# Fetched rows completed straight from the matmul accumulator, a deeper ring of gather buffers and a new order at the start of a two-layer graph attention kernel

## The chip, the cores and the metric

The kernel runs on one core of one Trainium2 chip. A core has a matrix engine (TensorE, in the rows PE for its matmuls and PEld for its weight loads), a vector engine (VectorE, DVE), a scalar engine (ScalarE, ACT), a general engine that also issues the indirect transfers (GpSimd, POOL), an engine that issues most other transfers (SyncE, SP) and 16 DMA engines. Each engine works through its own list of instructions in order, and they wait for each other by semaphores. Matmuls write to PSUM, an accumulator memory; everything else on the chip lies in SBUF. The metric is the device time of one execution in microseconds (us).

## The reference

N = 6250 nodes of 768 numbers, E = 100000 directed edges sorted by their destination, plus one self-loop per node. Cut to what matters:

```python
def gat_conv(x, src, dst, W, a_src, a_dst, bias, heads):
    h = (x @ W).reshape(n, heads, -1)
    alpha_s = (h * a_src[None]).sum(-1)
    alpha_d = (h * a_dst[None]).sum(-1)
    e = leaky_relu(alpha_s[src] + alpha_d[dst], 0.2)
    e = exp(e - segment_max(e, dst)[dst])
    alpha = e / (segment_sum(e, dst)[dst] + 1e-16)
    return segment_sum(h[src] * alpha[:, :, None], dst).reshape(n, -1) + bias

h = relu(layernorm(x))
h = relu(gat_conv(h, src, dst, W1, a_src1, a_dst1, b1, 4))   # 768 -> 256, 4 heads
h = relu(gat_conv(h, src, dst, W2, a_src2, a_dst2, b2, 1))   # 256 -> 256, 1 head
return x + relu(h @ Wm1 + bm1) @ Wm2 + bm2                   # 256 -> 768
```

All of it is float32.

## The kernel before

**Phase 1 (nodes).** The nodes lie in 49 tiles of 128. For each tile the kernel loads x (and for most tiles x transposed; the tiles in TURNED are transposed on the chip instead), takes means and variances (`moments`), spreads the means by a small matmul (`spread_means`), subtracts them (`centre`) and multiplies by W1 with 12 matmuls (L516). The row of a node (256 features and some factors, 268 numbers) stays in SBUF in `kept[tile]` for the whole layer and is also stored to a table in DRAM (L543).

**Layers (edges).** The edges stand in pairs of 2 x 128, two pairs to a group g, 196 groups to a layer. For every 128 edges GpSimd issues one indirect DMA that fetches their source rows from the table into one half of a buffer `G` (L718). The buffers form a ring, 20 deep. VectorE makes a one-hot matrix per group (`hot`, L746), the edge factors, and the product of rows and factors (`hw`: L796, L806, L808 in layer 1; L796, L799, L803 in layer 2). TensorE sums the edges of a destination with matmuls `o_ps` (L820). In layer 1 VectorE also makes the masks (L735) that layer 2 reads back. Layer 2 has the same form and ends with the two dense layers (y, L1190). When the sums of a node tile are complete, its row for layer 2 replaces the old one in `kept` and goes to the second table (L1074).

**Early rows.** While phase 1 still computes tiles, GpSimd already fetches rows for 30 pairs of layer 1 (SOON: pair i is fetched when the first SOON[i] tiles are in the table; `soon_rows`, L314, 60 indirect DMAs). Sources whose tile is not there yet get a row that is multiplied by zero later (`soon_ok`, from `soon_places`, L305 and L306, two small VectorE instructions per pair). The newest 16 of these buffers (SOON_HELD) stay in the ring; when one more is fetched, the oldest goes to DRAM (`soon_away`, L321). Before layer 1 all the rest follow, and `soon_back` reads each back when its turn comes. The rows that were not there are added in layer 1 from `kept`: VectorE compares the sources with node numbers (`soon_hits`, L338, up to 8 tiles in one instruction, called a part here), TensorE multiplies these matrices by the tiles of `kept` into one PSUM tile called `missing` (`soon_missing`, L351, two matmuls per tile; there is one such PSUM tile), ScalarE copies the sum to SBUF (`soon_out`, L356, into `soon_m`, three of them), and VectorE computes row * soon_ok + soon_m in place (`soon_whole`, L361). Between the layers the same is done for 10 pairs of layer 2 with names that begin with `next` (L381, L414, L420, L425).

**What sets the order.** The order on each engine is that of the code. In layer 1 each iteration g does, for VectorE, the `hot` of the group, at times a mask or a `mine`, then the steps that the table SOON_DOES holds for g, in the order of SOON_ORDER, then the edges of the pairs. SOON_DOES is made from SOON_GROUP: the group `at` in which a pair is used, and before it one part per group. For each of the two halves k of the pair, part j has its `hits` in group g-1 and its `missing` in group g; after the last part, `out` stands in group g+1 and both `whole` stand in group `at`. Towards the end of a layer the ring is made to skip buffers and GpSimd may be only two groups ahead (L941).

Of the kernel before, what the change touches and what calls it, by code (L numbers as in the profile page):

```python
# [17 lines left out]
P = 128  # L18
# [32 lines left out]
SOON_FROM, SOON_HELD = min(SOON), 16  # L51
# [3 lines left out]
TURNED = frozenset({0, 1, 31, 32, 34, 35, 37, 38, 40, 41, 43, 44, 46, 47})  # L55
# [15 lines left out]
for i, at in enumerate(SOON_GROUP):  # L71
    todo = [(2 * i + t, k) for t in range(2) for k in range(len(portions(SOON[i])))]
    for j, (k, part) in enumerate(todo):
        g = at - 1 - len(todo) + j
        SOON_DOES.setdefault(g - 1, []).append(("hits", k, part))
        SOON_DOES.setdefault(g, []).append(("missing", k, part))
        if part == len(portions(SOON[i])) - 1:
            SOON_DOES.setdefault(g + 1, []).append(("out", k, part))
            SOON_DOES.setdefault(at, []).append(("whole", k, part))
    SOON_DOES.setdefault(max(at - 5 - len(todo), 0), []).append(("sources", i, 0))  # L80
SOON_ORDER = ("whole", "out", "missing", "hits", "sources")
# [12 lines left out]
def kernel(  # L94
# [56 lines left out]
    nc.vector.tensor_copy(iota_ps, iota)  # L151
    nc.vector.tensor_copy(nid_ps, nid)
# [84 lines left out]
    def edge_places(ones):  # L237
# [3 lines left out]
        nc.sync.dma_start(src_i, src_cols)  # L241
        yield
        yield
        soonest = sorted(range(len(SOON)), key=SOON.__getitem__)
        for i in range(0, len(SOON), 2):
            for k in soonest[i:i + 2]:
                soon_places(k)
            yield
        for to, of in ((dst_i, dst_cols), (dri, dst_rows)):
            nc.sync.dma_start(to, of)  # L250
            yield
            yield
# [28 lines left out]
    gp = edges_stack.enter_context(tc.tile_pool(name="gathered", bufs=2 * (AHEAD + 2)))  # L281
# [16 lines left out]
    soon_G, soon_of, soon_p, soon_hit, soon_m = {}, {}, {}, {}, {}  # L298
# [55 lines left out]
    def soon_out(pool, k):  # L354
        soon_m[k] = pool.tile([P, TW[1]], F32, name="soon_m", bufs=3)
        nc.scalar.activation(soon_m[k], soon_p.pop(k), AF.Copy)  # L356

    def soon_whole(G, k):
        i, t = divmod(k, 2)
        row = G[soon_pair[i]][:, t]  # L360
        nc.vector.scalar_tensor_tensor(row, row, soon_ok[:, i, t:t + 1], soon_m.pop(k),  # L361
                                       ALU.mult, ALU.add)
# [4 lines left out]
    next_G, next_of, next_p, next_hit, next_m = {}, {}, {}, {}, {}  # L367
# [49 lines left out]
    def next_out(pool, i, t):  # L417

        next_m[i, t] = pool.tile([P, TW[2]], F32, name="next_m", bufs=2)
        nc.scalar.activation(next_m[i, t], next_p.pop((i, t)), AF.Copy)  # L420

    def next_whole(G, i, t):

        row = G[next_pair[i]][:, t]
        nc.vector.scalar_tensor_tensor(row, row, next_ok[:, i, t:t + 1], next_m.pop((i, t)),  # L425
                                       ALU.mult, ALU.add)

    def next_steps(g, pool, sm, G):

        for i, at in enumerate(NEXT_GROUP):  # L430
            if g == at - 10:
                next_sources(pool, i)
            for t in range(2):
# [5 lines left out]
                if g == first + 1:  # L439
                    next_out(sm, i, t)  # L440
                if g == at:
# [4 lines left out]
    with tc.tile_pool(name="w1p", bufs=1) as wp, tc.tile_pool(name="x1", bufs=6) as xp, \  # L446
# [62 lines left out]
        def features1(i):  # L509
# [3 lines left out]
            for k in range(KI):  # L513
                if (i, k) == (1, 2):
                    spread_means(2)
# [41 lines left out]
        nc.sync.dma_start(w1[:, :, :HID], W1.rearrange("(k p) f -> p k f", p=P))  # L557
        for i in range(1, 5):
# [13 lines left out]
        for i in range(NT):  # L572
# [5 lines left out]
            elif i == 1:  # L578
                centre(2)
                moments(3)  # L580
                spread_means(3)
                moments(4)
            else:
                if i + 3 < NT:
                    moments(i + 3)
                if i + 2 < NT:
                    spread_means(i + 2)
                if i + 1 < NT:
                    centre(i + 1)
# [22 lines left out]
            if i >= 10:  # L612
# [922 lines left out]
```

## Time and profile before

| | |
|---|---|
| median of 3 runs | 2086.26 us (2085.61 to 2087.27) |
| profiled execution, its own time | 2083.7 us |
| its span in the profile | 2081.8 us |
| TensorE busy (matmul) | 1767.1 us, 85% |
| VectorE busy | 1496.6 us, 72% |
| GpSimd busy | 1531.1 us, 74% |
| ScalarE busy | 453.6 us, 22% |
| phase 1 | 0 to about 171 us |
| layer 1 (first and last L718 there) | 170.93 to 1081.54 us |
| layer 2 (first L718) | from 1107.75 us |

How to read it: the shares are averages over stages that have different limits. GpSimd is the only engine whose list is full of one kind of instruction (L718), and these stand in a fixed order, so its position at a few places (first gather of phase 1, of layer 1, of layer 2) tells how far the whole program has come. Which engine waits for which in between is read from the waits, and how far one engine runs ahead of another from the time line.

### The profile page before, as it was taken

The numbers are of one execution on the slowest core, as the hardware profiler recorded it, in microseconds if no ns is written. First come the engines' busy times: TensorE is split into PE (matmuls) and PEld (weight loads), VectorE is DVE, ScalarE is ACT, GpSimd is POOL, SyncE is SP. The second block draws the span as 40 slices with busy tenths as digits, with TensorE's granted clock in tenths as the row PEclk, the third lists the DMA queues.
The fourth block names the chain that finished last, engine by engine and source line by source line (L and its number), as shares of the span: only waits on it lengthen the run. The fifth ranks groups of instructions, "written<-read, shape, count | busy, mean of one in ns | idle before, by whom it ended". The sixth has DMA issues, their size and how long they took to land.

```text
span 2081.8 us, 28821 instructions
## 1 busy us (share of the span) xinstructions
PE 1767.1 (85%) x8572; PEld 1335.8 (64%) x8574; DVE 1496.6 (72%) x4344; ACT 453.6 (22%) x1415; POOL 1531.1 (74%) x1669
## 2 busy tenths in 40 slices
PE   8985799999999999988874788887787787787777
PEld 7874687878888888766553555555555555554544
DVE  7845898989889999999973665665665565565554
ACT  5762111111111111222220111111111111111111
POOL 7267777777777777777777777777777777777774
PEclk9997999999999999998986898999999988898989
DMA  9999666666666666666659466556566556556553
GB/s 342 320 324 341 185 169 194 187 180 179 191 174 194 184 182 186 193 194 186 194 123 271 129 180 189 169 178 190 167 180 190 170 178 190 172 175 182 170 180 112
DMA packets 174908, 405.46 MB, mean 195 GB/s; under 512 B 37192, under 2 KB 61983, under 8 KB 174743
## 3 DMA queue, kind: packets, MB, share of 16 engines
q0 software_dynamic: 75040, 210.90, 38.6%
q1 hardware_dynamic: 98332, 191.14, 26.3%
q10 hardware_dynamic: 1370, 1.48, 0.3%
q8 instruction: 72, 1.18, 0.2%
q14 instruction: 94, 0.76, 0.1%
HBM read 334.24 MB, written 69.14 MB: 194 GB/s over the span
## 4 chain that ended last, share of the span: by engine, by line
PE 38%; DMA 20%; DVE 19%; issue 13%; POOL 9%; ACT 0%; DVEq 0%; SPq 0%; POOLq 0%; ACTq 0%
DMA G<-table,src_i 16%; PE o_ps L820 14%; PE missing L351 11%; POOL G L718 8%; PE h_ps L516 4%; PE y_ps L1190 4%; DVE hw L808 4%; DVE hot L746 3%; DVE soon_hit L338 2%; DVE iota_ps L796 2%; DVE hw L803 2%; DVE iota_ps L806 2%; DMA xTt<-in_xT 1%; DVE acc L831 1%; PE h_ps L1067 1%
## 5 line engine op out<-in xcount | busy, mean ns | idle before, releaser
L718 POOL DMA_INDIRECT G<-table,src_i x1484 | 1414.6, 953 | 452.1 <-issue 318.4
L820 PE MATMUL o_ps<-G,hw 128*128 128x258 f32 x1564 | 457.4, 425 | 208.6 <-DVE hw L803 206.0
L820 PEld LDWEIGHTS o_ps<-G,hw 128*128 128x128 f32 x1564 | 302.3, 207 | 338.2 <-DVE hw L803 280.8
L820 PE MATMUL o_ps<-hw,hot 128*128 128x260 f32 x1564 | 415.6, 407 | 65.5 <-DVE hw L808 62.8
L796 DVE TENSOR_TENSOR iota_ps<-G,iota_ps 128x8 f32<-128x8 f32 (+1 forms) x782 | 130.0, 166 | 398.4 <-DMA G<-table,src_i 387.6
L351 PE MATMUL missing<-kept,soon_hit 128*128 128x268 f32 x1648 | 398.4, 393 | 0.0
L820 PEld LDWEIGHTS o_ps<-hw,hot 128*128 128x128 f32 x1564 | 301.5, 199 | 145.4 <-DVE hw L808 91.4
L840 ACT ACTIVATE sum<-acc 32x260 f32<-32x260 f32 (+1 forms) x384 | 160.0, 417 | 1034.7 <-DVE acc L831 969.7
L351 PEld LDWEIGHTS missing<-kept,soon_hit 128*128 128x128 f32 x1648 | 310.7, 191 | 55.2
L803 DVE TENSOR_SCALAR hw<-iota_ps,dcol,w 128x128 f32<-128x128 f32 x782 | 284.9, 406 | 14.4
L808 DVE TENSOR_TENSOR hw<-G,iota_ps 128x520 f32<-128x520 f32 x391 | 272.0, 696 | 27.1
L1190 PE MATMUL y_ps<-wm,mT 128*128 128x384 f32 x392 | 183.2, 598 | 0.0
L516 PE MATMUL h_ps<-w,r 128*128 128x264 f32 (+1 forms) x588 | 140.0, 391 | 8.4 <-ACT r L506 8.1
L746 DVE TENSOR_TENSOR hot<-iota_ps,dcol 128x512 f32<-128x512 f32 x196 | 133.4, 681 | 0.0
L338 DVE TENSOR_TENSOR soon_hit<-soon_of,iota_ps 128x896 f32<-128x896 int32 (+6 forms) x126 | 128.0, 1016 | 2.4 <-PE missing L351 2.4
L516 PEld LDWEIGHTS h_ps<-w,r 128*128 128x128 f32 x588 | 109.5, 193 | 29.1 <-ACT r L506 9.6
L1190 PEld LDWEIGHTS y_ps<-wm,mT 128*128 128x128 f32 x392 | 78.1, 221 | 54.8 <-issue 29.2
L314 POOL DMA_INDIRECT G<-table,soon_i x60 | 57.9, 965 | 61.9 <-DMA table<-kept 41.3
L831 DVE SCALAR_TENSOR_TENSOR acc<-acc,keep,o_ps 128x260 f32<-128x260 f32 (+1 forms) x192 | 91.3, 476 | 0.9 <-PE o_ps L820 0.9
L356 ACT ACTIVATE soon_m<-missing 128x268 f32<-128x268 f32 x60 | 23.7, 394 | 264.5 <-PE missing L351 264.4
L806 DVE TENSOR_TENSOR iota_ps<-iota_ps,G 128x8 f32<-128x8 f32 x391 | 68.1, 174 | 13.4
L799 DVE TENSOR_TENSOR w<-iota_ps,G 128x2 f32<-128x2 f32 x391 | 62.2, 159 | 13.3
(424 smaller groups left out, 1369.9 us busy)
## 6 DMA issues: line engine op xcount, KB each, us to landing
xt<-in_x SPq DMA_DIRECT2D x96, 384.0 KB
drow<-dmod_d SPq DMA_DIRECT2D x49, 512.0 KB
mask_d<-mask SPq DMA_DIRECT2D x97, 256.0 KB
mask<-mask_d SPq DMA_DIRECT2D x97, 256.0 KB
G<-table,src_i POOLq DMA_INDIRECT x1484
out<-y SPq DMA_DIRECT2D x48, 384.0 KB
xTt<-in_xT SPq DMA_DIRECT2D x35, 384.0 KB
soon_d<-G SPq DMA_DIRECT2D x30, 268.0 KB
```

Source lines behind the costliest of these rows:

```text
L338: nc.vector.tensor_tensor(soon_hit[k, part][:, :b - a], soon_of[i][:, t * P:(t + 1) * P].unsqueeze(1).to_broadcast([P, b - a, P]), nid_ps[ ...
L351: nc.tensor.matmul(soon_p[k], hit[:, T - a], kept[T], start=(T == there), stop=(T == NT - 1))
L516: nc.tensor.matmul(h_ps[:, :n], r[:, k], w1[:, k, :n], start=(k == 0), stop=(k == KI - 1))
L718: nc.gpsimd.indirect_dma_start(out=G[k // 2][:n, k % 2], out_offset=None, in_=table[layer], in_offset=bass.IndirectOffsetOnAxis(ap=src_i[: ...
L746: nc.vector.tensor_tensor(hot[g][:, T[0]:T[0] + n], iota_ps.unsqueeze(1).to_broadcast([P, n, P]), dcol[:, k:k + n].unsqueeze(2).to_broadca ...
L796: nc.vector.tensor_mul(v, e2, v)
L803: nc.vector.tensor_scalar(hw[:, t], iota_ps, dcol[:, k:k + 1], w[:, t], ALU.is_equal, ALU.mult)
L808: nc.vector.tensor_mul(hw, Gp[:, :, :RW[1]].rearrange("p t (h c) -> p t h c", h=H), w.unsqueeze(3).to_broadcast([P, 2, H, C + 1]))
L820: nc.tensor.matmul(o_ps[u], l, r[:, :RW[layer]], start=(g % 2 == 0 and k == 0), stop=(g % 2 == 1 and k == tiles(g)[-1]))
L831: nc.vector.scalar_tensor_tensor(acc, run[0], keep[:, u % 2:u % 2 + 1], o_ps.pop(u), ALU.mult, ALU.add)
L840: nc.scalar.activation(done[t][r], acc[r], AF.Copy)
L1190: nc.tensor.matmul(y_ps, mT[:, j], wm2[:, j, s * half:(s + 1) * half], start=False, stop=(j == KH - 1))
```

## The change

- `soon_out` and `next_out` are removed. `soon_whole` and `next_whole` read the PSUM tile directly, and stand in group g+1 after the last part of their half (where `out` stood), no longer in group `at`.
- The ring of G has 24 buffers where it had 20, and SOON_HELD is 21 where it was 16.
- TURNED gets tiles 26 to 30 and 36 and loses 31, 35 and 37: 17 tiles are turned on the chip where 14 were, so 32 loads of x transposed are left of 35.
- W1 is loaded in two halves with the load of tile 1 between; the first six tiles have a new order of `centre`, `moments` and `spread_means`; two copies into PSUM move from the start to tile 5; the loads of the edge lists and with them `soon_places` start some tiles earlier (from i = 7 where it was 10).

```diff
-SOON_FROM, SOON_HELD = min(SOON), 16
+SOON_FROM, SOON_HELD = min(SOON), 21
-TURNED = frozenset({0, 1, 31, 32, 34, 35, 37, 38, 40, 41, 43, 44, 46, 47})
+TURNED = frozenset({0, 1, *range(26, 31), 32, 34, 36, 38, 40, 41, 43, 44, 46, 47})
...
         if part == len(portions(SOON[i])) - 1:
-            SOON_DOES.setdefault(g + 1, []).append(("out", k, part))
-            SOON_DOES.setdefault(at, []).append(("whole", k, part))
+            SOON_DOES.setdefault(g + 1, []).append(("whole", k, part))
...
-SOON_ORDER = ("whole", "out", "missing", "hits", "sources")
+SOON_ORDER = ("whole", "missing", "hits", "sources")
...
-    gp = edges_stack.enter_context(tc.tile_pool(name="gathered", bufs=2 * (AHEAD + 2)))
+    gp = edges_stack.enter_context(tc.tile_pool(name="gathered", bufs=24))
...
-    def soon_out(pool, k):
-        soon_m[k] = pool.tile([P, TW[1]], F32, name="soon_m", bufs=3)
-        nc.scalar.activation(soon_m[k], soon_p.pop(k), AF.Copy)
...
     def soon_whole(G, k):
         i, t = divmod(k, 2)
         row = G[soon_pair[i]][:, t]
-        nc.vector.scalar_tensor_tensor(row, row, soon_ok[:, i, t:t + 1], soon_m.pop(k),
+        nc.vector.scalar_tensor_tensor(row, row, soon_ok[:, i, t:t + 1], soon_p.pop(k),
                                        ALU.mult, ALU.add)
...
                 if g == first + 1:
-                    next_out(sm, i, t)
-                if g == at:
                     next_whole(G, i, t)
...
-        nc.sync.dma_start(w1[:, :, :HID], W1.rearrange("(k p) f -> p k f", p=P))
-        for i in range(1, 5):
+        for h in range(2):
+            ks = slice(h * (KI // 2), (h + 1) * (KI // 2))
+            nc.sync.dma_start(w1[:, ks, :HID], W1.rearrange("(k p) f -> p k f", p=P)[:, ks])
+            if h == 0:
+                fetch_x(1)
+        for i in range(2, 5):
...
                 spread_means(1)
                 centre(1)
                 moments(2)
-            elif i == 1:
-                centre(2)
-                moments(3)
-                spread_means(3)
-                moments(4)
+                spread_means(2)
+            elif i < 4:
+                centre(i + 1)
+                moments(i + 2)
+                spread_means(i + 2)
+                if i == 3:
+                    moments(6)
             else:
+                if i + 1 < NT:
+                    centre(i + 1)
+                if i + 2 < NT:
+                    spread_means(i + 2)
                 if i + 3 < NT:
                     moments(i + 3)
-                if i + 2 < NT:
-                    spread_means(i + 2)
-                if i + 1 < NT:
-                    centre(i + 1)
...
-            if i >= 10:
+            if i >= 7:
                 next(pieces, None)
```

VectorE of before around group 90 of layer 1, the last group but one before pair 183 (half k = 27 of the early rows) is used; `mine` is a node tile's own rows times their self-loop factors:

```order
L746 TENSOR_TENSOR hot<-iota_ps,dcol 128x512
L1038 TENSOR_TENSOR mine<-kept_137,own 128x260
L796 TENSOR_TENSOR iota_ps<-G,iota_ps 128x8
L806 TENSOR_TENSOR iota_ps<-iota_ps,G 128x8
L808 TENSOR_TENSOR hw<-G,iota_ps 128x520
```

The same engine and place of the changed kernel (its line numbers are about 11 lower):

```order
L735 TENSOR_TENSOR hot<-iota_ps,dcol 128x512
L1027 TENSOR_TENSOR mine<-kept_135,own 128x260
L350 SCALAR_TENSOR_TENSOR G<-G,soon_ok,missing_6005 128x268
L785 TENSOR_TENSOR iota_ps<-G,iota_ps 128x8
L795 TENSOR_TENSOR iota_ps<-iota_ps,G 128x8
L797 TENSOR_TENSOR hw<-G,iota_ps 128x520
```

The completion of k = 27 now stands ahead of the two `hw` of this group, and reads `missing`.

VectorE of before one group later, group 91:

```order
L1044 TENSOR_TENSOR all__6197<-mine,sum 128x260
L1057 RECIPROCAL rden<-all__6197 128x4
L1059 TENSOR_TENSOR o<-all__6197,rden 128x256
L746 TENSOR_TENSOR hot<-iota_ps,dcol 128x512
L735 TENSOR_SCALAR mask<-drow,pidx 128x1024
L361 SCALAR_TENSOR_TENSOR G<-G,soon_ok,soon_m 128x268 x2
L338 TENSOR_TENSOR soon_hit<-soon_of,iota_ps 128x768
```

The same in the changed kernel:

```order
L1033 TENSOR_TENSOR all__6159<-mine,sum 128x260
L1046 RECIPROCAL rden<-all__6159 128x4
L1048 TENSOR_TENSOR o<-all__6159,rden 128x256
L735 TENSOR_TENSOR hot<-iota_ps,dcol 128x512
L724 TENSOR_SCALAR mask<-drow,pidx 128x1024
L331 TENSOR_TENSOR soon_hit<-soon_of,iota_ps 128x768
```

Both completions are gone from group 91. The other half of the pair (k = 26) is completed three groups earlier, in group 87.

SyncE of before at the end of phase 1; `soon_d` is the place in DRAM for the early rows, `mask_d` that for the masks:

```order
L321 DMA soon_d<-G 128x536
L543 DMA table_97<-kept_162 128x268
L543 DMA table_97<-kept_163 128x268
L1026 DMA w_2137<-in_W 128x2x256
L194 DMA w2T<-in_W2T 128x2x256
L675 DMA drow<-dmod_d 128x2048 x3
L321 DMA soon_d<-G 128x536 x16
L675 DMA drow<-dmod_d 128x2048
L737 DMA mask_d<-mask 128x1024 x4
```

The same in the changed kernel:

```order
L314 DMA soon_d<-G 128x536
L523 DMA table_95<-kept_160 128x268
L523 DMA table_95<-kept_161 128x268
L1015 DMA w_2148<-in_W 128x2x256
L191 DMA w2T<-in_W2T 128x2x256
L664 DMA drow<-dmod_d 128x2048 x3
L314 DMA soon_d<-G 128x536 x21
L664 DMA drow<-dmod_d 128x2048
L726 DMA mask_d<-mask 128x1024 x4
```

Of the 30 stores of early rows 9 are left inside phase 1 where 14 were, and 21 stand ahead of the first stores of masks where 16 did. The order on GpSimd is the same in both kernels.

## Rows read from the trace of the kernel before

**Rows 1.** Position of GpSimd: time line (start, duration, [idle before <- ended by]).

```profile
88.54 1.14 POOL L314 DMA_INDIRECT G<-table,soon_i  x1 [37.73 <-DMA table<-kept]
...
111.00 0.94 POOL L314 DMA_INDIRECT G<-table,soon_i  x1 [2.32 <-DMA table<-kept]
...
150.78 0.94 POOL L314 DMA_INDIRECT G<-table,soon_i  x1 [4.49 <-DMA soon_d<-G]
...
170.93 0.95 POOL L718 DMA_INDIRECT G<-table,src_i  x1 [0.30 <-issue]
...
1082.71 0.95 POOL L381 DMA_INDIRECT G<-table,next_i  x1 [0.30 <-issue]
...
1107.75 0.95 POOL L718 DMA_INDIRECT G<-table,src_i  x1 [0.30 <-issue]
```

**Rows 2.** Costliest groups of the page: busy, mean ns | idle before.

```profile
L718 POOL DMA_INDIRECT G<-table,src_i x1484 | 1414.6, 953 | 452.1 <-issue 318.4
L351 PE MATMUL missing<-kept,soon_hit 128*128 128x268 f32 x1648 | 398.4, 393 | 0.0
L831 DVE SCALAR_TENSOR_TENSOR acc<-acc,keep,o_ps 128x260 f32<-128x260 f32 (+1 forms) x192 | 91.3, 476 | 0.9 <-PE o_ps L820 0.9
L356 ACT ACTIVATE soon_m<-missing 128x268 f32<-128x268 f32 x60 | 23.7, 394 | 264.5 <-PE missing L351 264.4
```

**Rows 3.** Busy time by stage (layer 1 from 300 us, layer 2).

```profile
core 0: us, PE busy (x) PEld busy (x) DVE busy (x) ACT busy (x) POOL busy (x), PEclk, DMA share, GB/s
300.00:1085.00 785.00, 739.88 (x3773) 604.89 (x3773) 715.55 (x1810) 152.88 (x538) 595.73 (x622) 0.97 0.65 183
1108.00:2082.00 974.00, 764.61 (x3541) 520.04 (x3542) 556.25 (x1958) 171.40 (x457) 722.51 (x762) 0.90 0.59 175
```

**Rows 4.** What VectorE waited for, 240 to 900 us: total, times, longest.

```profile
DVE G L361 <- ACT soon_m L356: 15.7, 7, 3.8
DVE soon_hit L338 <- PE missing L351: 2.4, 3, 1.0
```

**Rows 5.** Time line of VectorE, groups 90 and 91.

```profile
615.46 0.42 DVE L1038 TENSOR_TENSOR mine<-kept,own 128x260 f32<-128x260 f32 x1
...
620.20 0.49 DVE L361 SCALAR_TENSOR_TENSOR G<-G,soon_ok,soon_m 128x268 f32<-128x268 f32 x1
623.90 0.50 DVE L361 SCALAR_TENSOR_TENSOR G<-G,soon_ok,soon_m 128x268 f32<-128x268 f32 x1 [3.21 <-ACT soon_m L356]
...
625.78 0.70 DVE L808 TENSOR_TENSOR hw<-G,iota_ps 128x520 f32<-128x520 f32 x1
...
627.65 0.69 DVE L808 TENSOR_TENSOR hw<-G,iota_ps 128x520 f32<-128x520 f32 x1
```

**Rows 6.** ScalarE at the end of the matmuls of k = 27.

```profile
623.47 0.39 ACT L356 ACTIVATE soon_m<-missing 128x268 f32<-128x268 f32 x1 [8.65 <-PE missing L351]
```

**Rows 7.** TensorE after them.

```profile
623.27 3.67 PE L820 MATMUL o_ps<-hw,hot 128*128 128x260 f32 x16
```

**Rows 8.** End of layer 1 on VectorE, and the start of layer 2 there.

```profile
1084.72 0.70 DVE L808 TENSOR_TENSOR hw<-G,iota_ps 128x520 f32<-128x520 f32 x1
...
1115.53 0.17 DVE L796 TENSOR_TENSOR iota_ps<-G,iota_ps 128x2 f32<-128x2 f32 x1 [17.35 <-DMA G<-table,src_i]
```

**Rows 9.** What VectorE waited for, 200 to 300 us.

```profile
DVE iota_ps L796 <- DMA G<-table,src_i: 6.1, 6, 3.2
```

**Rows 10.** What VectorE waited for, 170 to 200 us.

```profile
DVE mask L735 <- DMA mask_d<-mask: 5.8, 1, 5.8
```

**Rows 11.** TensorE at tile 3 of phase 1.

```profile
19.72 2.86 PE L516 MATMUL h_ps<-w,r 128*128 128x256 f32 x12 [1.95 <-ACT r L506]
```

**Rows 12.** VectorE and GpSimd in phase 1, 45 to 46 us.

```profile
45.71 0.16 DVE L305 TENSOR_SCALAR soon_ok<-src_i 128x2 f32<-128x2 int32 x1
45.79 1.19 POOL L530 TENSOR_TENSOR ha<-kept,a1b 128x512 f32<-128x512 f32 x1
45.90 1.10 DVE L306 TENSOR_TENSOR soon_i<-src_i,soon_ok 128x2 int32<-128x2 int32 x1
```

More of the change, by code (lines that the diff above doesn't have):

```diff
@@ L150 @@
     iota_ps, nid_ps = both_ps[:, :P], both_ps[:, P:P + NT]
-    nc.vector.tensor_copy(iota_ps, iota)
-    nc.vector.tensor_copy(nid_ps, nid)
     eps_c = const.tile([P, 1], F32, name="eps_c")
@@ L240, in edge_places @@
         dri = ones.tile([NCH, CH], I32, name="dri")
-        nc.sync.dma_start(src_i, src_cols)
-        yield
-        yield
+        for to, of in ((src_i, src_cols), (dst_i, dst_cols), (dri, dst_rows)):
+            nc.sync.dma_start(to, of)
+            yield
         soonest = sorted(range(len(SOON)), key=SOON.__getitem__)
@@ L247, in edge_places @@
                 soon_places(k)
[L248 to L251, printed above, removed]
             yield
@@ L297 @@
     soon_d = dram.tile([len(SOON), P, 2 * TW[1]], F32, name="soon_d")
-    soon_G, soon_of, soon_p, soon_hit, soon_m = {}, {}, {}, {}, {}
+    soon_G, soon_of, soon_p, soon_hit = {}, {}, {}, {}
     soon_pair = {i: pair for pair, i in SOON_AT.items()}
@@ L366 @@
     next_d = dram.tile([len(NEXT), P, 2, TW[2]], F32, name="next_d")
-    next_G, next_of, next_p, next_hit, next_m = {}, {}, {}, {}, {}
+    next_G, next_of, next_p, next_hit = {}, {}, {}, {}
     next_pair = {i: pair for pair, i in NEXT_AT.items()}
@@ L415, in next_missing @@
                              stop=(T == NT - 1))
-    def next_out(pool, i, t):
-        next_m[i, t] = pool.tile([P, TW[2]], F32, name="next_m", bufs=2)
-        nc.scalar.activation(next_m[i, t], next_p.pop((i, t)), AF.Copy)
     def next_whole(G, i, t):
         row = G[next_pair[i]][:, t]
-        nc.vector.scalar_tensor_tensor(row, row, next_ok[:, i, t:t + 1], next_m.pop((i, t)),
+        nc.vector.scalar_tensor_tensor(row, row, next_ok[:, i, t:t + 1], next_p.pop((i, t)),
                                        ALU.mult, ALU.add)
@@ L513, in features1 @@
             for k in range(KI):
-                if (i, k) == (1, 2):
-                    spread_means(2)
                 nc.tensor.matmul(h_ps[:, :n], r[:, k], w1[:, k, :n], start=(k == 0), stop=(k == KI - 1))
@@ L577 @@
                 moments(2)
-            elif i == 1:
-                centre(2)
-                moments(3)
-                spread_means(3)
-                moments(4)
-            else:
+                spread_means(2)
[5 more added lines that the diff above has]
+                    moments(6)
+            else:
+                if i + 1 < NT:
+                    centre(i + 1)
+                if i + 2 < NT:
+                    spread_means(i + 2)
                 if i + 3 < NT:
                     moments(i + 3)
-                if i + 2 < NT:
-                    spread_means(i + 2)
-                if i + 1 < NT:
-                    centre(i + 1)
+            if i == 5:
+                nc.vector.tensor_copy(iota_ps, iota)
+                nc.vector.tensor_copy(nid_ps, nid)
             if i == 0:
```

## The prediction

> **What bounds the kernel now.** I read the page's engine shares and costliest groups first, then the time line of GpSimd, then the waits of VectorE, and last the time lines of both engines around one early pair.
>
> The reader is to see in the time line of GpSimd that it has no holes [rows 1]: from its first early gather at 88.54 us it issues one indirect DMA after another, 0.95 us of work and 0.30 us of "issue", so one per 1.25 us, with two gaps above that, 2.32 us (a row of the table is not stored) and 4.49 us (a ring buffer is not yet copied away). No wait for a free buffer shows in the layers: the idle time of L718 is 1484 times about 0.30 us [rows 2]. Layer 2 begins at 1107.75 us, and there GpSimd sets the end: 762 instructions of 1.25 us fill 953 of 974 us, while VectorE and TensorE have slack [rows 3], and VectorE had to wait 17.35 us for the first rows [rows 8]. So the time is where GpSimd stands at 1107.75 us, plus a tail that the change leaves as it is.
>
> The second thing to see is how little room the other engines have in layer 1: from 300 to 1085 us TensorE is busy 740 and VectorE 716 of 785 us [rows 3]. VectorE waits for almost nothing: 15.7 us at L361 and 2.4 us at L338 between 240 and 900 us [rows 4]. Groups with a part of early rows (12 to 16 matmuls `missing`, 0.39 us each) are bound by TensorE, groups without by VectorE, and the two engines pass the lead back and forth. That works because VectorE runs up to two groups ahead of TensorE. The last product ends at 1084.72 + 0.70 = 1085.4 us [rows 8], 22 us before GpSimd starts layer 2; GpSimd has 20 gathers (25 us) in between [rows 1].
>
> **The change part by part.**
>
> *Phase 1.* It can bring GpSimd forward. The 4.49 us gap is the ring's: buffers that are held now (21 for 16) need not be copied out first, so I count it as gone. TensorE waited 1.95 us at tile 3 [rows 11]; the new order of the first tiles and the split load can take that, and the stores from which the early gathers wait come earlier by at most as much. The 2.32 us gap waits for a table row, so it moves with the tiles and stays. Sum: 4.5 + 2.0 = 6.5 us, and a little for three fewer loads and five fewer stores in a stage whose DMA is full: 7 us, so L718 first at 164 instead of 170.93 us. Ends: 0 (another row or buffer is late in its place) and 9 us (the 2.32 us go too).
> Against it stands the earlier `soon_places`. The trace has one of its instructions at 1.10 us where its sibling takes 0.16 us, and it began 0.11 us after a GpSimd instruction of 1.19 us and ended with it [rows 12]. Starting two tiles earlier puts about four more of the 60 into that stretch, 4 x 0.94 = 3.8 us of VectorE if every one is caught. VectorE has slack there, so I take nothing off, and keep 3.8 us in the lower end.
> The Trainium skill, "SBUF — State Buffer", section "Who interferes with whom", says that VectorE and GpSimd take a shared port pair as an exclusive lock for a whole instruction, and that the loser blocks. That row agrees; by the rule the 3.8 us would be paid in full, and the gain would be 3 us instead of 7.
>
> *Completion from PSUM.* The 60 copies on ScalarE (23.7 us in all) [rows 2] were on an engine that is 22% busy, so their removal is worth nothing in itself. The reading price on VectorE is the same: the nearest row with a PSUM operand, L831, takes 476 ns for 260 columns [rows 2], and the completion from SBUF takes 0.49 us for 268 [rows 5]. What changes is who waits, and where. VectorE now has the completion right after the `hot` of group g+1, where ScalarE stood before. ScalarE could afford it: it waited 264.4 us in all for these 60 sums [rows 2]. VectorE can't: behind its wait stand the `hw` of the group, and TensorE waits for those.
>
> Take k = 27, the last half of pair 183. VectorE is through with `mine` of group 90 at 615.46 + 0.42 = 615.88 us [rows 5]. The last matmul of that sum is done at 623.47 us, when ScalarE starts the copy [rows 6]. In the new order VectorE stands 7.6 us at this place. From 615.88 to 620.20 us it did 4.3 us of work, which comes after it now. In the trace it waits 3.21 us one group later and ends the second completion at 624.40 us; in the new order it is at the same point at 623.47 + 0.49 + 4.32 = 628.3 us. So 3.9 us are lost. TensorE feels them: at 623.27 us it has four pairs of `o_ps` waiting and takes 3.67 us for them [rows 7], two of these need the `hw` that now begin at 624 us, and the next groups have no matmuls `missing` behind which VectorE could catch up.
>
> I read the same two times at all 60 places. For both halves VectorE would come too early at most of them, by 125 us in all. Most of that is no loss: where another part follows at once, TensorE is the bound and VectorE only waits with it. It is a loss where the parts of a pair end and light groups follow. Nine of the 30 pairs have a lead there that is not won back: 7.2, 4.0, 6.0, 7.2 (the pair above, without the second completion that no longer stands there), 3.0, 4.3, 3.0, 2.9 and 1.9 us, together 39.5 us. Of that the kernel before pays 15.7 us already [rows 4], so VectorE's list becomes 39.5 - 15.7 = 24 us longer. Ends: 0 (TensorE is late by its own work and VectorE's waits fall into time that it has anyway) and 39.5 us (the old waits come back at other places). I take 24, which is worked out place by place.
>
> *What this does to GpSimd.* VectorE starts layer 1 with GpSimd 7 us earlier as well: the wait for the mask store (5.8 us) and the waits for gathered rows (6.1 us) are the room for it [rows 9, 10]. Net, its last product ends 24 - 7 = 17 us later, at 1102.4 us. GpSimd may be 24 buffers ahead in the middle, but the ring narrows at the end: the last gathers of layer 1 are let out only when VectorE is about three groups from its end. At 1.87 us for a pair (627.65 - 625.78) [rows 5] six pairs are 11 us; 20 gathers of layer 2 follow, 25 us; so layer 2 can't begin before the last product plus about 15 us. Before, that was 1085.4 + 15 = 1100.4 us and GpSimd came at 1107.75 us, with 7 us to spare. After, it is 1102.4 + 15 = 1117.4 us: 9.7 us later than before.
>
> *Layer 2.* The same edit for 20 halves changes no time: GpSimd is the bound there, and its order is the same. With the deeper ring VectorE and TensorE keep their slack. I count 0, with 2 us as the upper end for a wait at the last of them.
>
> Sum: the profiled execution took 2083.7 us with a span of 2081.8 us, 1.9 us lying around it; with 9.7 us more it is 2093.4 us. The median of the runs shown is 2.6 us above that execution, so I predict 2086.3 + 9.7 = 2096.0 us.
>
> **The rivals.**
> - *GpSimd stays the bound (faster).* The new waits of VectorE fall into the room that the deeper ring gives, and layer 2 starts as early as GpSimd can: 7 us earlier, 2079 us. For it: GpSimd never waits in the trace, four more buffers are two more pairs, and the room at 1107.75 us is 7 us before and 14 us with the start moved. It holds as long as VectorE's list becomes less than about 10 us longer. Against it: k = 27 alone costs 3.9 us, and eight more are like it.
> - *The two cancel.* VectorE loses 10 to 19 us, and layer 2 starts between 4 us earlier and 4 us later: 2082 to 2090 us. For it: leads that I count as lost may in part be won back behind the next pair's parts, where TensorE is the bound again.
> - *No gain at the start.* Phase 1 gives back on VectorE what it wins, or a store is late in the place of the buffer: L718 starts at 170 us, and the loss of 24 us stands alone: last product at 1109.4 us, layer 2 at 1124.4 us, 16.7 us later, 2103 us. For it: the four or more instructions beside GpSimd [rows 12], and 21 stores ahead of the masks where 16 stood.
> - *The copies' time counts.* If TensorE waits for ScalarE before it may start the next `missing`, dropping a copy of 0.394 us 60 times is worth up to 23.7 us. Against it: L351 shows no idle time before its matmuls in 1648 [rows 2], so no more than a few us; I count it to the first rival.
>
> **How the numbers follow.** My forecast has 45% (layer 2 between 4 and 14 us later), no gain at the start or a greater loss 13%, the two cancel 20%, GpSimd stays the bound 22%. A difference of 0.2%, 4.2 us, is about what a measurement of this kernel can tell from no change. Slower by more than that: 45 + 13 = 58%; within it 20%; faster 22%. The range that holds 8 in 10 goes from the first rival's 2078 to 2103 us; my forecast's own range is 2090 to 2100 us.
>
> **What would show it.** L718 first at about 164 us and the 4.49 us gap gone: the start is right. In layer 1 a wait of VectorE for TensorE's `missing` at the completion, 40 us or more in place of 15.7, and TensorE waiting for `hw` behind it; from some pair past the middle, GpSimd with gaps above 0.30 us that VectorE ends; the first gather of layer 2 at about 1117 us: the coupling is right. If GpSimd shows no gaps and layer 2 starts near 1101 us, the first rival is right and my reading of the lost leads is wrong. If L718 starts at 170 us, the part on phase 1 is wrong. Layer 2 should last as long as before, 974 us from its first gather; if not, the cost that I took as zero is not.

## The result, and the profile after

The changed kernel took 2107.4 us (2106.1 to 2112.9), the kernel before 2085.9 us beside it: a ratio of 1.0108, with a 95% interval of 1.0089 to 1.0128. It is slower by 21.5 us, where 9.7 us were forecast (2096.0 us, range 2078 to 2103 us). The profiled execution took 2106.1 us with a span of 2104.3 us.

The time line of GpSimd in the changed kernel, at the places of [rows 1]:

```profile
85.46 1.32 POOL L307 DMA_INDIRECT G<-table,soon_i  x1 [34.62 <-DMA table<-kept]
...
108.31 0.95 POOL L307 DMA_INDIRECT G<-table,soon_i  x1 [1.64 <-DVE brest L210]
...
137.03 1.03 POOL L307 DMA_INDIRECT G<-table,soon_i  x1 [3.64 <-DVE mv L447]
...
167.69 0.97 POOL L707 DMA_INDIRECT G<-table,src_i  x1 [0.30 <-issue]
...
777.13 0.94 POOL L707 DMA_INDIRECT G<-table,src_i  x1 [2.37 <-DVE iota_ps L785]
...
787.82 0.94 POOL L707 DMA_INDIRECT G<-table,src_i  x1 [0.71 <-DVE iota_ps L785]
...
801.56 0.94 POOL L707 DMA_INDIRECT G<-table,src_i  x1 [1.26 <-DVE hw L797]
...
858.95 0.95 POOL L707 DMA_INDIRECT G<-table,src_i  x1 [1.92 <-DVE hw L797]
...
897.06 0.95 POOL L707 DMA_INDIRECT G<-table,src_i  x1 [0.55 <-DVE hw L797]
...
1102.92 0.88 POOL L707 DMA_INDIRECT G<-table,src_i  x1 [20.65 <-DVE iota_ps L785]
1104.10 1.07 POOL L370 DMA_INDIRECT G<-table,next_i  x1 [0.30 <-issue]
...
1129.29 0.95 POOL L707 DMA_INDIRECT G<-table,src_i  x1 [0.30 <-issue]
```

GpSimd starts layer 1 3.2 us earlier than before, and layer 2 21.5 us later (1129.29 for 1107.75 us). All of the result is there: from that gather to the end of the span it is 975.0 us now and was 974.1 us. GpSimd has six new waits in layer 1, all named after VectorE. Five short ones, 6.8 us in all, stand between 777 and 897 us; the sixth, 20.65 us, stands before the very last gather of the layer. The 20 gathers for layer 2 follow that one without a gap. The end of layer 1 on VectorE, which answers to [rows 8]:

```profile
1102.37 0.28 DVE L706 MEMSET G<- 128x268 f32 x1
...
1111.38 0.69 DVE L797 TENSOR_TENSOR hw<-G,iota_ps 128x520 f32<-128x520 f32 x1
```

The MEMSET clears the half empty buffer of the last edges, and the gather starts 0.27 us after its end. In the kernel before the same clearing came in time: it began at 1074.67 us, and GpSimd reached the last gather only at 1081.54 us, without a wait.

```profile
1074.67 0.28 DVE L717 MEMSET G<- 128x268 f32 x1
```

The last product of VectorE ends at 1112.1 us, where it ended at 1085.4 us before.

The groups of the two lines that meet at `missing` (busy, mean ns | idle before), against [rows 2]:

```profile
L344 PE MATMUL missing<-kept,soon_hit 128*128 128x268 f32 x1648 | 400.1, 394 | 2.9 <-DVE G L350 2.9
L350 DVE SCALAR_TENSOR_TENSOR G<-G,soon_ok,missing 128x268 f32<-128x268 f32 x60 | 29.4, 489 | 57.6 <-PE missing L344 57.4
```

The completion takes 489 ns from PSUM, as it took 0.49 us from SBUF [rows 5], but VectorE waits 57.4 us for it in layer 1, in 33 places, where it waited 15.7 us in 7 [rows 4]. TensorE in turn waits longer for the products `hw` of layer 1, 86.0 us where it was 62.8 us (L820 and L808 are lines of the kernel before; total, times, longest):

```profile
DVE G L350 <- PE missing L344: 57.4, 33, 3.9
...
PE o_ps L820 <- DVE hw L808: 62.8, 65, 6.7
...
PE o_ps L809 <- DVE hw L797: 86.0, 83, 7.4
```

A measure that hangs little on phase 1 is used below: the **length of layer 1 on VectorE**, from GpSimd's first gather of the layer to the end of VectorE's last product. It is 1085.42 - 170.93 = 914.5 us before and 1112.07 - 167.69 = 944.4 us after: 30 us more. It is good to 2 or 3 us: the ring alone, which leaves the completions as they were, has 916.8 us. Below, the two halves of a pair are called first (k even) and second (k odd), and a light group is a group without a part of early rows.

### The profile page after: what moved, and what is told of

Read it like the earlier page. It is cut to its first block, busy times and chain, and to the rows that moved or that the text cites. A ratio compares the mean times of both kernels' runs of the same rounds, so it can differ in the third digit from the quotient of the medians.

```text
span 2104.3 us, 28630 instructions
## 1 busy us (share of the span) xinstructions
PE 1774.7 (84%) x8588; PEld 1336.6 (64%) x8589; DVE 1496.5 (71%) x4344; ACT 422.7 (20%) x1338; POOL 1532.6 (73%) x1669
## 4 chain that ended last, share of the span: by engine, by line
PE 45%; DMA 20%; DVE 18%; issue 10%; POOL 7%; ACT 0%; DVEq 0%; SPq 0%; POOLq 0%; ACTq 0%
PE o_ps L809 17%; DMA G<-table,src_i 16%; PE missing L344 13%; POOL G L707 6%; PE y_ps L1179 5%; DVE hw L797 4%; PE h_ps L496 3%; DVE hot L735 2%; DVE soon_hit L331 2%; DVE iota_ps L785 2%; DMA table<-kept 2%; DVE iota_ps L795 1%; PE h_ps L1056 1%; DVE hw L792 1%; DVE acc L820 1%
## 5 line engine op out<-in xcount | busy, mean ns | idle before, releaser
L809 PEld LDWEIGHTS o_ps<-G,hw 128*128 128x128 f32 x1564 | 307.3, 209 | 324.4 <-DVE hw L792 262.8
L809 PEld LDWEIGHTS o_ps<-hw,hot 128*128 128x128 f32 x1564 | 296.1, 197 | 177.1 <-DVE hw L797 122.1
L1179 PEld LDWEIGHTS y_ps<-wm,mT 128*128 128x128 f32 x392 | 80.4, 227 | 57.4 <-issue 36.0
L820 DVE SCALAR_TENSOR_TENSOR acc<-acc,keep,o_ps 128x260 f32<-128x260 f32 (+1 forms) x192 | 91.3, 476 | 1.4 <-PE o_ps L809 1.2
L350 DVE SCALAR_TENSOR_TENSOR G<-G,soon_ok,missing 128x268 f32<-128x268 f32 x60 | 29.4, 489 | 57.6 <-PE missing L344 57.4
```

Source lines behind the costliest of these rows:

```text
L809: nc.tensor.matmul(o_ps[u], l, r[:, :RW[layer]], start=(g % 2 == 0 and k == 0), stop=(g % 2 == 1 and k == tiles(g)[-1]))
L820: nc.vector.scalar_tensor_tensor(acc, run[0], keep[:, u % 2:u % 2 + 1], o_ps.pop(u), ALU.mult, ALU.add)
L1179: nc.tensor.matmul(y_ps, mT[:, j], wm2[:, j, s * half:(s + 1) * half], start=False, stop=(j == KH - 1))
```

## The experiments

All ratios are against the kernel before, measured beside it, with 95% intervals. Times of the kernel before lay between 2080.7 and 2085.9 us, but for two sets of runs in which it took about 2610 us (told last).

**Completion from PSUM alone.** The kernel before, with this part of the diff (and the same for `next_whole`) and nothing else:

```diff
-            SOON_DOES.setdefault(g + 1, []).append(("out", k, part))
-            SOON_DOES.setdefault(at, []).append(("whole", k, part))
+            SOON_DOES.setdefault(g + 1, []).append(("whole", k, part))
...
-                                       soon_m.pop(k), ...)
+                                       soon_p.pop(k), ...)
```

> The kernel before with the completion from PSUM alone (copies removed, completions moved to group g+1); ring of 20, 16 held and phase 1 as before. Theory (the new waits of VectorE are the whole loss): L718 first at 171 us as before, VectorE waits 50 us or more at the completions, its last product about 24 us later than 1085.4 us, GpSimd's last gather of layer 1 held until then, layer 2 first at about 1132 us, time 2110 us. Rival (the deeper ring, the 21 held buffers or phase 1 cost the time): 2086 us.

Measured: 1.0121 (1.0104 to 1.0138), layer 2 first at 1128.03 us, VectorE waits 55.4 us at the completions, length 941.5 us, 27 us more than before. The theory holds, the rival falls: this part alone is the loss.

```profile
DVE G L360 <- PE missing L350: 55.4, 31, 3.7
```

```profile
1128.03 0.95 POOL L715 DMA_INDIRECT G<-table,src_i  x1 [0.30 <-issue]
```

**All but that.** The changed kernel with copies and places of before put back.

> The changed kernel with the copies on ScalarE and both completions in their old groups put back: ring, held buffers, turned tiles and phase 1 alone. Theory: GpSimd is the bound again, starts layer 1 3.2 us earlier (167.7 us) and keeps that to the end: layer 2 first at 1104.5 us, time 2083 us. Rival (something in these parts costs time): 2090 us or more.

Measured: 0.9988 (0.9978 to 0.9997), length 914.5 us as in the kernel before. Its first gathers of layer 1 and layer 2:

```profile
165.43 1.03 POOL L719 DMA_INDIRECT G<-table,src_i  x1 [0.30 <-issue]
...
1102.13 0.95 POOL L719 DMA_INDIRECT G<-table,src_i  x1 [0.30 <-issue]
```

What GpSimd wins at the start (5.5 us in this execution) it has at the start of layer 2 too (5.6 us). Ring, held buffers and phase 1 cost nothing.

**The ring alone.** The kernel before with 24 buffers and 21 held.

> The kernel before with the ring of 24 and 21 held buffers alone. The prediction counted the gap of 4.49 us before a gather of phase 1 as gone by this. Theory (the gap's place is taken by a wait for a table row, since the gathers of the last tiles can't come before the tiles): the gap of 4.49 us goes, L718 first at 168 to 171 us, time within 2 us of the kernel before. Rival (as predicted): L718 first at 166 us, time 4 us below the kernel before.

Measured: 1.0000 (0.9991 to 1.0009). The first early gather is where it was, the gap of 4.49 us is gone, and layer 1 starts at 165.66 us:

```profile
88.29 1.15 POOL L314 DMA_INDIRECT G<-table,soon_i  x1 [37.39 <-DMA table<-kept]
...
165.66 1.31 POOL L718 DMA_INDIRECT G<-table,src_i  x1 [0.30 <-issue]
```

In the trace that is the rival's start, and in the time the theory's. The start of layer 1 came between 164.1 and 168.8 us in all other profiles of these chips, whatever was in them, so a single profile's start is no measure of 3 us here. The first early gather is steadier: 84.9 to 85.9 us in the nine profiles with the new phase 1, 88.0 to 88.5 us in the three without.

**Place without PSUM.** The copies on ScalarE are back, but VectorE completes in group g+1, behind them. Against "all but that" the edit is this, with `out` ahead of `whole` in SOON_ORDER:

```diff
-            SOON_DOES.setdefault(at, []).append(("whole", k, part))
+            SOON_DOES.setdefault(g + 1, []).append(("whole", k, part))
```

> The changed kernel with the copies on ScalarE put back, but each completion on VectorE left at its new place in group g+1, behind the copy: place without PSUM. Theory (the place costs, not the memory): as slow as the changed kernel or a few us slower, since each wait now includes the copy of 0.39 us; 21 to 27 us above the kernel before, layer 2 first at 1129 to 1135 us. Rival (reading PSUM on VectorE, or holding the one PSUM tile until VectorE comes, costs): no slower than the kernel before.

Measured: 1.0188 (1.0173 to 1.0204), length 963.0 us; slower than the changed kernel by more than expected. VectorE's wait:

```profile
DVE G L355 <- ACT soon_m L350: 69.3, 39, 3.8
```

It is the place in VectorE's list that costs, not that VectorE reads PSUM: with the copy between, each wait ends later still.

**The clearing of the last buffer on GpSimd.**

```diff
-                        nc.vector.memset(G[k // 2][:, k % 2], 0.0)
+                        nc.gpsimd.memset(G[k // 2][:, k % 2], 0.0)
```

> The changed kernel, with the clearing of the last, half empty gather buffer on GpSimd instead of VectorE. In the changed kernel the last gather of layer 1 waited 20.65 us and ended its wait after that clearing (1102.37 us on VectorE). Theory (this one instruction lets VectorE's delay through to GpSimd): the wait goes, the 20 gathers between the layers are issued by 1109 us, and layer 2 then waits for the last row of the second table, whose store is issued at 1119.65 us: first gather at about 1122 us instead of 1129.3, time 2100 us. Rival 1 (the gathers between the layers wait for rows of the second table in any case): 2107 us. Rival 2 (that wait was all of the loss): 2085 us.

Measured: 1.0085 (1.0068 to 1.0101). The last gather of layer 1 and the first of layer 2:

```profile
1082.54 0.87 POOL L707 DMA_INDIRECT G<-table,src_i  x1 [0.27 <-POOL G L706]
...
1125.93 0.95 POOL L707 DMA_INDIRECT G<-table,src_i  x1 [13.46 <-DMA next_d<-G]
```

The wait of 20.65 us is gone, and 13.46 us of another stand in its place. The 20 gathers between the layers start at 1083.72 us and are issued by 1112.5 us, so they do not wait for the last rows of the second table (rival 1); and the wait of 20.65 us was not all of the loss (rival 2). The time alone does not tell the theory from rival 1: this interval and that of the changed kernel (1.0089 to 1.0128) overlap. SyncE's list shows what can hold the first gather of layer 2: the stores `next_d` that the wait is named after stand behind the store of the last node row.

```profile
1120.34 0.32 SPq L1063 DMA_DIRECT2D table<-kept  x1
```

That store is issued 7.3 us after VectorE's last product of the layer (1113.02 us here). So GpSimd is tied to the end of the layer in two ways, and the clearing is the later one by some 4 us in these two profiles: counted from the last product, layer 2 begins after 12.9 us here and after 17.2 us in the changed kernel. Whether the row or the buffers end the wait here was not separated.

**Nine completions back.** The changed kernel, with the nine second halves on which the forecast's sum rested one group later. They still read PSUM.

```diff
+            late = k in (7, 15, 21, 27, 31, 35, 39, 41, 43)
-            SOON_DOES.setdefault(g + 1, []).append(("whole", k, part))
+            SOON_DOES.setdefault(at if late else g + 1, []).append(("whole", k, part))
```

> The changed kernel with nine of the 60 completions (k = 7, 15, 21, 27, 31, 35, 39, 41, 43, the second halves that are followed by light groups and had a lead of 1.9 us or more) moved one group later, to the group in which they stood before; all 60 still read PSUM. Theory (only leads that are followed by light groups are lost): VectorE's list gets nearly 24 us shorter again, layer 2 starts at 1104 to 1110 us, time 2082 to 2088 us. Rival (each of the 60 waits costs its share): 9/60 of the 42 us of new waits, 6 us, time 2101 us.

Measured: 1.0014 (1.0004 to 1.0023), length 923.0 us: 21 of the 30 us come back from 9 of 60 instructions. The first gather and the last product of the layer:

```profile
168.71 1.13 POOL L708 DMA_INDIRECT G<-table,src_i  x1 [0.30 <-issue]
```

```profile
1090.97 0.69 DVE L798 TENSOR_TENSOR hw<-G,iota_ps 128x520 f32<-128x520 f32 x1
```

What is left of it in the time is again the one wait for the clearing, as the next run shows:

```profile
1082.93 0.87 POOL L708 DMA_INDIRECT G<-table,src_i  x1 [6.61 <-DVE iota_ps L786]
```

**Both of these.** Nine completions back and the clearing on GpSimd.

> The changed kernel with both edits of the second round's two best: the nine completions (k = 7, 15, 21, 27, 31, 35, 39, 41, 43) one group later, and the last buffer cleared by GpSimd. With the nine alone GpSimd still waited 6.61 us for that clearing. Theory (what was left of the loss went through that one wait): the wait goes and layer 2 starts at about 1103 us, time 3 us below the kernel before, as with the copies put back. Rival (the other 51 completions cost the rest by themselves): 2 to 3 us above the kernel before, as with the nine alone.

Measured: 0.9981 (0.9972 to 0.9991). The time is as expected though layer 2 began later than that, at 1107.68 us after a wait of 2.57 us, in its profile. It is the fastest version found, and not separable from the one with the copies put back.

**Nine others back.** As above, with k = 3, 5, 11, 13, 17, 19, 23, 25, 29, the second halves that parts of the next pair follow at once.

> The changed kernel with nine other second halves one group later (k = 3, 5, 11, 13, 17, 19, 23, 25, 29): those that the parts of the next pair follow at once. Their raw leads are as large as those of the first nine (6.4 us at 13, 7.0 us at 19). Theory (waits there are spent while TensorE is the bound): little is won back, less than 6 us; 15 to 22 us above the kernel before. Rival (every wait counts): as good as the first nine, 2 to 6 us above the kernel before.

Measured: 1.0259 (1.0243 to 1.0274), the slowest of all, length 976.3 us. Theory and rival are both wrong: nothing comes back, and 32 us more are lost. What VectorE and TensorE waited for:

```profile
DVE G L351 <- PE missing L345: 86.5, 32, 7.4
```

```profile
PE missing L345 <- DVE G L351: 22.5, 14, 4.7
```

There is one PSUM tile for `missing`. Where the next part follows at once, TensorE can't begin it before VectorE has read the tile, one group later now (22.5 us of waiting, 2.9 us in the changed kernel); and VectorE waits for TensorE at the next place (86.5 us, 57.4 us there). So a completion can move back only where no part follows at once.

**The nine alone.** The reverse: the nine from PSUM in group g+1, the other 51 through copies in their old groups.

> The changed kernel with the nine completions (k = 7, 15, 21, 27, 31, 35, 39, 41, 43) alone read from PSUM in group g+1, and the other 51 by the copy in their old group. Theory (the nine alone cost what moving them back won, 21 us of VectorE): on a chip of 2083 us 932 to 938 us from the first gather of layer 1 to VectorE's last product, time 6 to 12 us above the kernel before. Rival (the 60 completions cost only together, each delay feeding the next): 920 us or less, time within 3 us of the kernel before. On a chip of 2610 us: between the first halves alone (1.0144 and 1.0169) and none, so 1.002 to 1.012.

Measured: 1.0125 (1.0102 to 1.0148), length 944.7 us, more than either said: nine early completions cost as much as sixty. The length's two ends, and VectorE's waits at the nine completions and at the other 51:

```profile
165.10 0.95 POOL L722 DMA_INDIRECT G<-table,src_i  x1 [0.30 <-issue]
```

```profile
1109.12 0.69 DVE L812 TENSOR_TENSOR hw<-G,iota_ps 128x520 f32<-128x520 f32 x1
```

```profile
DVE G L358 <- PE missing L348: 48.7, 9, 7.7
...
DVE G L358 <- ACT soon_m L353: 2.7, 3, 1.1
```

VectorE at k = 27 (`mine` of group 90, then the completion), and TensorE behind it:

```profile
617.68 0.42 DVE L1042 TENSOR_TENSOR mine<-kept,own 128x260 f32<-128x260 f32 x1
625.76 0.49 DVE L358 SCALAR_TENSOR_TENSOR G<-G,soon_ok,missing 128x268 f32<-128x268 f32 x1 [7.67 <-PE missing L348]
```

```profile
625.56 4.05 PE L824 MATMUL o_ps<-hw,hot 128*128 128x260 f32 x16
...
632.90 1.14 PE L824 MATMUL o_ps<-hw,hot 128*128 128x260 f32 x4 [2.97 <-DVE hw L812]
```

7.67 us were worked out as 7.6 from [rows 5, 6]. TensorE uses up its four pairs, as [rows 7] led to expect, and then stands 2.97 us before the next. The same place in the changed kernel:

```profile
623.74 0.42 DVE L1027 TENSOR_TENSOR mine<-kept,own 128x260 f32<-128x260 f32 x1
626.89 0.49 DVE L350 SCALAR_TENSOR_TENSOR G<-G,soon_ok,missing 128x268 f32<-128x268 f32 x1 [2.73 <-PE missing L344]
```

With all 60 early, the completions before this one have already taken part of VectorE's lead; the wait is shorter here, and there are more of them.

**The first halves alone.** The 30 first halves from PSUM in group g+1, the second halves through copies.

> First halves alone from PSUM in group g+1, a third time, for a chip of 2083 us. Theory A (they cost next to nothing there): 914 to 918 us from the first gather of layer 1 to VectorE's last product, time 3 us below the kernel before. Theory B (they cost the rest of the loss): 922 us or more, time between 3 below and 2 us above. On a chip of 2610 us: 1.014 to 1.017, as twice.

Measured: 0.9991 (0.9981 to 1.0000), length 923.5 us. VectorE's wait and GpSimd's:

```profile
DVE G L357 <- PE missing L347: 32.0, 16, 4.0
```

```profile
1079.40 0.87 POOL L721 DMA_INDIRECT G<-table,src_i  x1 [5.82 <-DVE iota_ps L799]
```

By the length theory B holds: they cost 9 us of VectorE (the first halves stand two to four groups earlier than before), the same as what was left with the nine back (923.0 us). The time doesn't show it: layer 2 begins at 1105.87 us, 1.9 us earlier than before. GpSimd's earlier start and the room at the end of the layer can take it up; that was not measured apart.

**Where the kernel before took 2610 us.** In two sets of runs, noted as on chips 0 and 7, the kernel before took 2609.5 and 2612.4 us. Chip 0 is also noted with 2080.7 us, so it is not shown that one chip, or the chip at all, makes the difference. Eight runs stand there, two of each of four kernels: first halves alone, second halves alone, all 19 second halves that at least two light groups follow moved back (with the clearing on GpSimd), and the new phase 1 alone.

> The changed kernel with the 30 first halves completed from PSUM in group g+1 and the 30 second halves by the copy in their old group. Theory A (first halves cost next to nothing, since the parts of the second half follow at once): 914 to 918 us from the first gather of layer 1 to VectorE's last product, time 3 us below the kernel before. Theory B: 922 us or more, time between 3 below and 2 us above the kernel before.

> The reverse: the 30 second halves from PSUM in group g+1, the 30 first halves by the copy in their old group. Theory A: nearly all of the loss is here, 938 to 944 us from the first gather of layer 1 to VectorE's last product, time 16 to 21 us above the kernel before. Theory B: 930 to 937 us, time 6 to 14 us above the kernel before.

> The changed kernel with all 19 second halves that at least two light groups follow one group later (the nine and ten with small leads), and the last buffer cleared by GpSimd. From GpSimd's first gather of layer 1 to VectorE's last product there passed 914.5 us in the kernel before, 944.4 us in the changed one, 922.9 and 925.9 us with the nine late; so some 10 us of VectorE are still lost. Theory A (the ten other light ends cost them): 915 to 918 us. Theory B (the first halves, which all stand two or three groups earlier now, cost them): 922 us or more. Time in either case 3 us below the kernel before, since GpSimd is the bound again.

> The kernel before with the new order of the first tiles, the split load of W1, the earlier edge lists and the new set of turned tiles alone (ring of 20, 16 held, copies kept). Theory (these bring the 2 to 3 us that the start gains; the ring alone measured no difference): first early gather at about 85.5 us instead of 88.5, L718 first at 167 to 169 us, time 2 to 3 us below the kernel before. Rival (it takes both parts): time within 1 us of the kernel before.

| kernel | first run | second run |
|---|---|---|
| first halves alone | 1.0144 (1.0101 to 1.0188) | 1.0169 (1.0124 to 1.0214) |
| second halves alone | 1.0232 (1.0187 to 1.0276) | 1.0213 (1.0169 to 1.0257) |
| light ends moved back | 1.0034 (1.0009 to 1.0058) | 1.0007 (0.9980 to 1.0034) |
| new phase 1 alone | 1.0008 (0.9986 to 1.0031) | 0.9992 (0.9958 to 1.0025) |

The second runs had the same expectations. These were for times of about 2083 us, and the lengths can't be set beside theirs. TensorE's largest waits before `missing` and `o_ps` have no engine or transfer behind them that the profile shows (phase 1 alone, first run, up to 1400 us); the next one has ScalarE's copies:

```profile
PE missing L345 <- issue: 76.6, 66, 11.4
PE o_ps L821 <- issue: 75.2, 68, 6.4
...
PE missing L345 <- ACT soon_m L350: 42.1, 11, 20.1
```

In its second run the copies lead before `missing` (62.2 us for 49.7 us without a releaser). In these two sets both halves cost time, the second more. With the light ends moved back nearly all of it is gone, though the first halves stand early in that kernel too; whether the clearing on GpSimd or the missing copies do that was not separated. The new phase 1 can't be told from none in either run, so which part of the change wins the start in the time is open; the 0.12% of "all but that" is all that was measured of it.

## Why the prediction was wrong

**What bounds the kernel** was right. GpSimd's position at the start of layer 2 sets the end, and the rest of layer 2 kept its length within 1 us, the 20 completions there included (0 was counted, 2 as upper end).

**The mechanism** was right in VectorE's list: the place of the completion couples VectorE to TensorE, and the copies and the price of reading PSUM don't matter. The signs named for it came: VectorE's wait of 40 us or more (57.4 us), TensorE's longer wait for `hw`, and gaps on GpSimd past the middle that VectorE ends (the five between 777 and 897 us). It was wrong in the last step, how the delay gets from VectorE to GpSimd at the end of layer 1, and the size was wrong. Layer 2 began 21.5 us later for 9.7 us forecast, 11.8 us off, from three terms of the sum:

- **The coupling, 24 us, measured 30 us** (length 944.4 - 914.5; 27 us in the run with this part alone). This is the largest term, and the one that was mis-sized most. The nine places were right, as the two runs with the nine show (21 us back when they alone move, 30 us lost when they alone stand early). The sum of their leads was not. Their waits, alone, were 7.29, 5.81, 5.91, 7.67, 6.66, 6.56, 3.67, 3.26 and 1.84 us, in the order of the forecast's list, 48.7 us in all for 39.5. Six agree within 0.7 us. The sum fails at k = 15, 31 and 35: 5.8, 6.7 and 6.6 us where 4.0, 3.0 and 4.3 us had been taken; 7.7 of the 9.2 us are these three. In the trace of before the sums at these places are done 5.8, 4.0 and 5.9 us after VectorE comes there, so the forecast had counted part of each lead as won back. At k = 15 that is all of the error, and at k = 35 most of it; at k = 31 most of it is that the lead itself grew, from 4.0 to 6.7 us, and why is open. Of the 18.1 us of old waits [rows 4], 15.7 of which were set against the leads, 4.3 us stayed (2.7 at other completions, 1.6 at `soon_hit`). 48.7 + 4.3 - 18.1 is 34.9 us of added waits, and 30 us of added length.
- **The start, 7 us, measured 3.2 us** in these two profiles. The tiles come 3 us earlier, more than the 2.0 us that were taken for them, and the 4.49 us gap is gone, but waits of 1.64 and 3.64 us stand elsewhere, both named after VectorE. As the start differs from one profile to the next by as much as this term, its 3.8 us are the least certain of the three. The forecast's own lower end named this ("another row or buffer is late in its place").
- **Last product plus 15 us, measured plus 17.2 us** (1129.29 - 1112.07). The forecast's own parts, 25 - 11, make 14, not 15, so its working is 3.2 us short. The gather that is held starts 9.2 us before the last product, not 11, and it is one more that has to be issued after the wait: 21 gathers of 1.256 us, 26.4 us, not 25. The path was wrong too. The step says that the ring lets out the last gathers of layer 1 only when VectorE is about three groups from its end. With the clearing on GpSimd the last gather was issued at 1082.54 us, 30.5 us before VectorE's last product, so the ring does not hold it; in the changed kernel one instruction in VectorE's list does, the clearing of the last buffer. Without it the next tie, at the store of the last row, comes some 4 us sooner. That 15 us came so near is luck.

5.9 + 3.8 + 2.2 = 11.9 us, which is the difference; the three add up by their definition, so this shows where the error lies and not why.

**That first halves cost nothing** ("TensorE is the bound and VectorE only waits with it") was wrong for VectorE, which loses 9 us by them alone, and right for the time of 2083 us (where the kernel before took 2610 us they cost 1.4 to 1.7%). The two losses don't add up (30 and 9 alone, 30 together). I read that as a lead that can be lost only once; no run shows it by itself.

**The Trainium skill's rule** on the shared port ("SBUF — State Buffer", section "Who interferes with whom"), which spoke for a gain of 3 us instead of 7, came nearer to the measured start than the forecast did; but the blocked `soon_places` are not shown to be the reason. More of these 60 instructions did take over 0.3 us (eight, where four did), but together they took 13.2 us for 11.5 before, 1.7 us more and not 3.8. All of them had ended by 81.4 us, and the first gather behind them came 3.1 us earlier than before. No run kept the new phase 1 with the old `soon_places`.

**The rivals.** "GpSimd stays the bound" and "the two cancel" fell; what they describe is what the kernel does with nine completions back. The room of the first was put at 14 us, and its limit at about 10 us; by the forecast's own numbers VectorE moves with the start as well, and the room stays 7 us. "No gain at the start" had the size nearest to the measured one (16.7 us), by a cause that only half took place: the start did gain something, and most of the rest came from the coupling. "The copies' time counts" fell: without them the kernel is slower, and with copies and old places back the length is 914.5 us as before.

## What to carry to other kernels

When two nearly full engines pass a lead back and forth, ask of each instruction that reads another engine's result how long the reader would stand there, and what stands behind it; an engine that is idle anyway (here ScalarE, 22% busy) may be worth keeping as the one that waits. Such a stop costs where light work follows for the producer, and a buffer released late costs where heavy work follows, so the same move can be right at nine places and wrong at nine others. And look for the single instruction through which a delay reaches the engine that sets the end: here a clearing of one buffer passed the delay on as a wait of 20.65 us, and with that wait taken away the next tie stood some 4 us behind, so little came back.

## What was not expected of the hardware

In two sets of runs the kernel before took 2609.5 and 2612.4 us where it took 2081 to 2086 us in the others. In the first profile of the new phase 1 alone GpSimd's gathers took as long there as elsewhere (955 ns, 953 in [rows 2]), and VectorE's products too (696 ns). But up to 1400 us TensorE stood 76.6 and 75.2 us before the matmuls of `missing` and `o_ps` with no releaser in the profile, where all its matmuls together have under 9 us of that in the kernels before and after. These are 152 us of the 330 us by which layer 1 is longer there. TensorE's mean granted clock was 0.831, where it was 0.926 in the kernel before; whether that is a cause or follows from the waits is not shown, nor what TensorE waited for.
